# Zero padding the z product and the B and C product to full 128 x 128 tiles

## The chip, the cores and the metric

The kernel runs on one core of one Trainium2 chip. The metric is the device time of one launch in microseconds (us). A measured time is given as the median of several runs; a profile is one further execution, with its own time. PE is the matrix engine (TensorE), DVE the vector engine, ACT the scalar engine, POOL the GpSimd engine, SP the engine that here only issues DMAs. PEld stands for PE's weight loads.

## What is computed

The input is `x` of shape (4, 128, 64, 64). Layer 0 normalises it, passes it through a depthwise convolution, a GELU and a 1 x 1 product, and then through a selective state space model (Mamba). Layer 1 is attention with four heads over the 4096 pixels of each image, and a mixture of eight experts of which each pixel takes two. The change lies in the state space model. Its reference, cut to what matters:

```python
def _mamba(xc, in_proj_w, conv1d_w, conv1d_b, x_proj_w, ...):
    xz = u @ in_proj_w.T                      # (L, 32) by (32, 128)
    xin, z = jnp.split(xz, 2, axis=-1)        # 64 channels each
    xin = silu(depthwise_conv(xin, conv1d_w) + conv1d_b)
    x_dbl = xin @ x_proj_w.T                  # 2 + 16 + 16 columns
    dt, Bm, Cm = jnp.split(x_dbl, [R, R + N], axis=-1)
    delta = softplus(dt @ dt_proj_w.T + dt_proj_b)
    dA = jnp.exp(delta[..., None] * A)
    dBu = delta[..., None] * Bm[:, :, None, :] * xin[..., None]
    # h = dA * h + dBu, step by step over the pixels;  y = sum over n of h * C
    y = ... + D_skip * xin
    return y * silu(z) @ out_proj_w.T
```

The 128 channels of a pixel are cut into four chunks of 32, and the model runs on each chunk on its own. `in_proj_w` gives 64 channels to `xin` and 64 to `z` from the 32 of a chunk. All of this is in f32.

## The kernel before

**Tiles and stages.** An image of 4096 pixels is cut into eight blocks of 512 pixels (`BLK`). With four images that is 32 blocks. Channels lie on partitions. The four chunks are taken as two pairs, p = 0 and p = 1: pair p holds the channels on partitions 64p to 64p + 63, which are two chunks of 32, and one pair makes 2 x 64 = 128 rows of `xin`, of `z` and of the state. So the function `inputs(b, i, p)` (L659), which makes everything that the recurrence needs, runs 64 times, once for each image, block and pair.

**What `inputs` does.** It is a generator; each `yield` ends a stage.

- Stage one: PE makes the convolved input (`inxc` from `pairs`, two products that are summed in the PSUM tile `ps_Y`) and then `z` into the PSUM tile `ps_X`. For `z` it takes 64 rows of the weights `inz` and 64 rows of `xn`, those of the pair.
- Stage two: ACT makes `xin` (Silu of the first) and `zs` (Silu of the second).
- Stage three: PE makes the B and C columns (`wbc` from `xin`, 64 columns of weights, so 64 rows of the PSUM tile `pb`), and then `wdt` from `xin`.
- Stage four: ACT copies the 64 rows of `pb` to `bc`, which is sent to memory as `bcd`, and computes the softplus for `delta` in several steps (Abs, Exp, Ln, Relu). The stages after that let DVE finish `delta` and `du`.

A product of f32 operands is issued as two passes, so each call has two matmul instructions for `z` and two for B and C.

**What runs beside it.** The recurrence goes over units of two states: `fetched` brings the B or C rows from memory (`rows<-bcd`), `decayed` makes the factors on ACT (`da`), `driven` multiplies on DVE (`h<-rows,du`), `scan` runs the recurrence on DVE (`h<-da,state,h`), `read` multiplies with C on DVE (`hc`), and `turned_on` sums `hc` in PSUM with PE (`y<-ident,hc`). Attention of the image before runs in the same slots: PE makes scores (`sc<-qs,ks`, one pass each, 128 columns of weights), ACT takes exponentials (`pT<-sc`), and PE multiplies with the values one slot later (`av<-pT,v`, weights of 64 columns, two products beside each other in the two column halves).

**What sets the order.** Every instruction of the main loop goes through a small class `Queue` (its calls are recorded at L406), which chains each engine's instructions in the order of the program text. No scheduler moves them. In each slot the main loop issues, for PE, in this order: scores, one stage of a lane's task, `y` products, another stage, the `av` products, another stage. Two lanes, X and Y, hold tasks; `inputs` is in lane Y, and its products use the one PSUM buffer of each lane (`work("X")`, `work("Y")`). So the `pb` product waits until the last reader of lane X's buffer is done. In many calls with p = 0 that is the task that makes keys and queries (`closed`): its products `w_wkn` and `w_wqn` are read by DVE as `hi` and `lo`.

The weights are laid out by `_laid_out` on the host and loaded once at the start, `inz` and `wbc` on ACT's DMA queue.

Of the kernel before, what the change touches and what calls it, by code (L numbers as in the profile page):

```python
# [17 lines left out]
P = 128  # L18
C = 128
EPS = 1e-5  # L20
BLK = 512
NT = BLK // P
IMG = 64
DI = 64
NST = 16
# [11 lines left out]
def conv_mamba_attn_moe_kernel(ctx: ExitStack, tc: tile.TileContext, t: dict):  # L37
# [15 lines left out]
    def load(name, shape=None, src=None, eng=nc.sync, pool=const):  # L53
        src = t[name] if src is None else src
        w = pool.tile(list(shape or src.shape), F32, name=f"w_{name}")
        eng.dma_start(out=w, in_=src)
        return w
# [20 lines left out]
    inx, xdt, dtT, alog = (load(k, pool=scratch, eng=late) for k in ("inx", "xdt", "dtT", "alog"))  # L78
# [3 lines left out]
    inz, wbc, wout, projT = (load(k, eng=late) for k in ("inz", "wbc", "wout", "projT"))  # L82
# [14 lines left out]
    for j in range(4):  # L97
        r = slice(DI * (j % 2), DI * (j % 2) + DI)
# [313 lines left out]
    def mm(out, lhsT, rhs, start=True, stop=True):  # L412
        tensor.matmul(out, lhsT=lhsT, rhs=rhs, start=start, stop=stop)

    def summed(ps, terms):
        for i, (lhsT, rhs) in enumerate(terms):
            mm(ps, lhsT, rhs, i == 0, i == len(terms) - 1)
# [4 lines left out]
    def send(out, in_, slots=1):  # L422
        outgoing.append([slots, out, in_])
# [24 lines left out]
    def work(lane, shape=None):  # L448
        return ps_work.tile(shape or [P, BLK], F32, tag=f"work{lane}", name=f"ps_{lane}")

    def tmp(lane, name, shape=None):
        return side.tile(
            shape or [P, BLK], F32, tag=f"tmp{lane}", name=name, bufs=6 if lane == "X" else 4
        )
# [204 lines left out]
    def inputs(b, i, p):  # L659

        xn, pairs = xn_of[b, i], pairs_of[b, i]
        r = slice(DI * p, DI * p + DI)
        while held:
            yield
            yield
        held.add("in")
        ps = work("Y")
        summed(ps, [(inxc[:, j, :], pairs[:, p, 2 * j : 2 * j + BLK]) for j in range(2)])
        pz = work("X")
        mm(pz, inz[r, :], xn[r, 3 : 3 + BLK])  # L670
        yield
        xin = mix.tile([P, BLK], F32, name="xin", bufs=2)
        scalar.activation(xin, ps, AF.Silu, bias=cb)
        zs = mix.tile([P, BLK], F32, name="zs", bufs=4)
        scalar.activation(zs, pz, AF.Silu)
        yield

        pb = work("X")
        mm(pb[0:DI, :], wbc, xin)
        ps = work("Y")  # L680
        mm(ps, wdt, xin)
        yield
        held.clear()
        bc = tmp("Y", "bc")[0:DI, :]
        scalar.copy(bc, pb[0:DI, :])
        bcd = dram.tile([2, NST // 2, 2, 2 * BLK], F32, name="bcd", bufs=4)
        send(bcd.rearrange("c n k (m q) -> (c n k m) q", m=2), bc)

        e = tmp("Y", "e")
        scalar.activation(e, ps, AF.Abs, bias=dtb)  # L690
        scalar.activation(e, e, AF.Exp, scale=-1.0)
        ln = tmp("Y", "ln")
        scalar.activation(ln, e, AF.Ln, bias=1.0)
        delta = mix.tile([P, BLK], F32, name="delta", bufs=2)
        scalar.activation(delta, ps, AF.Relu, bias=dtb)
        yield
        yield

        du = mix.tile([P, BLK], F32, name="du", bufs=2)
        lost = du  # L700
        vector.tensor_scalar(lost, e, 1.0, -1.0, ALU.add, ALU.add)
        vector.tensor_sub(lost, e, lost)
        vector.tensor_add(ln, ln, lost)
        vector.tensor_add(delta, delta, ln)
        vector.tensor_mul(du, delta, xin)
        in_of[b, i, p] = xin, zs, delta, du, bcd
        done.add(("in", b, i, p))
        yield
# [603 lines left out]
    for k in range(-2, len(blocks)):  # L1312
        if 0 <= k:
            b, i = blocks[k]
            Y.append((("in", b, i, 1), inputs(b, i, 1), [("scan", *blocks[k - 1], 1)] if k else []))
        if k + 2 < len(blocks):
            b, i = blocks[k + 2]
            if k + 2 == 0 or i > 0:
                upper(k + 2)
        if 0 <= k + 1 < len(blocks):  # L1320
            b, i = blocks[k + 1]
            below = [("y0", b, i + 1)] if i < NB - 1 else []
            Y.append((("xn", b, i), conv(b, i), before(k + 1, 3) + below))
            Y.append((
                ("in", b, i, 0), inputs(b, i, 0),
                before(k + 1, 2) + ([("scan", *blocks[k], 0)] if k >= 0 else []),
            ))

        if 0 < k + 2 < len(blocks) and blocks[k + 2][1] == 0:
            upper(k + 2)  # L1330
# [113 lines left out]
def _laid_out(i):  # L1444
    import numpy as np

    f = {k: np.asarray(a) for k, a in i.items()}
    c0 = {k[len("L0_conv_") :]: a for k, a in f.items() if k.startswith("L0_conv_")}

    def col(a):  # L1450
        return a.reshape(-1, 1)

    def row(a):
        return a.reshape(1, -1)


    def twice(a):
        return np.repeat(a, 2, axis=0)

    z = np.zeros((P, P), np.float32)  # L1460
    inx, inz = z.copy(), z.copy()
    wout = np.zeros((P, 2, P), np.float32)
    wbc = np.zeros((P, 2, NST // 2, 2, 2), np.float32)
    xdt, dtT = np.zeros((4, P), np.float32), np.zeros((4, P), np.float32)
    for c in range(2):
        d = slice(c, P, 2)
        for p in range(2):
            s = slice(64 * p + 32 * c, 64 * p + 32 * c + 32)
            inx[s, d] = c0["in_proj_w"][:DI].T
            inz[s, d] = c0["in_proj_w"][DI:].T  # L1470
            wout[d, p, s] = c0["out_proj_w"].T

        wbc[d, c] = c0["x_proj_w"][2:].reshape(2, NST // 2, 2, DI).transpose(3, 1, 0, 2)
        xdt[2 * c : 2 * c + 2, d] = c0["x_proj_w"][:2]
        dtT[2 * c : 2 * c + 2, d] = c0["dt_proj_w"].T

    w = f["L1_attn_W_qkv"].reshape(C, NH, DH, 3)
    bw = f["L1_attn_b_qkv"].reshape(NH, DH, 3)
    wq, wk = np.zeros((C, 2, P), np.float32), np.zeros((C, 2, P), np.float32)
    bq, bk = np.zeros((P, 2), np.float32), np.zeros((P, 2), np.float32)  # L1480
    for h in range(NH):
        s = slice(64 * (h % 2), 64 * (h % 2) + DH)
        wq[:, h // 2, s], wk[:, h // 2, s] = w[:, h, :, 0], w[:, h, :, 1]
        bq[s, h // 2], bk[s, h // 2] = bw[h, :, 0], bw[h, :, 1]

        bk[64 * (h % 2) + DH, h // 2] = 1.0
    x = f["x"]
    laid = {
        "x": x.reshape(x.shape[0], C, -1),

        "xtok": x.reshape(x.shape[0], C, -1, P).transpose(0, 3, 2, 1).reshape(x.shape[0], P, -1),
        "gmat": np.kron(np.eye(C // 4), np.full((4, 4), 0.25)).astype(np.float32),
        "lnw": col(c0["ln_w"]), "lnb": col(c0["ln_b"]),
        "lcw": col(c0["lc_ln_w"]), "lcb": col(c0["lc_ln_b"]),
        "fc1w": c0["lc_fc1_w"].reshape(C, 9), "fc1b": col(c0["lc_fc1_b"]),
        "fc2T": c0["lc_fc2_w"].T, "fc2b": col(c0["lc_fc2_b"]),
        "inx": inx, "inz": inz,
        "cw": twice(c0["conv1d_w"]).T,
        "cb": col(twice(c0["conv1d_b"])),
        "xdt": xdt, "dtT": dtT, "dtb": col(twice(c0["dt_proj_b"])),  # L1500
        "wbc": wbc.reshape(P, -1), "alog": twice(c0["A_log"]),
        "dsk": col(twice(c0["D_skip"])), "wout": wout,
        "projT": c0["proj_w"].T, "projb": row(c0["proj_b"]), "skip": c0["skip_scale"],
        "wq": wq, "wk": wk, "wv": w[:, :, :, 2].reshape(C, C),
        "bq": bq, "bk": bk, "bv": row(bw[:, :, 2]),
        "wqn": w[:, :, :, 0].reshape(C, C), "wkn": w[:, :, :, 1].reshape(C, C),
        "bqn": col(bw[:, :, 0]), "bkn": col(bw[:, :, 1]), "bvc": col(bw[:, :, 2]),
        "wp": f["L1_attn_W_proj"], "bp": row(f["L1_attn_b_proj"]),
        "rw": f["L1_ffn_router_w"], "rb": f["L1_ffn_router_b"],
        "ew": f["L1_ffn_expert_w"].transpose(1, 0, 2), "eb8": f["L1_ffn_expert_b"],  # L1510
    }
    return {k: np.ascontiguousarray(a) for k, a in laid.items()}
# [17 lines left out]
```

## Time and profile before

| what | value |
|---|---|
| median of 3 runs | 5217.45 us (5217.27 to 5228.61) |
| the profiled execution: its own time | 5213.97 us |
| the profiled execution: span from first to last instruction | 5211.8 us |
| mean granted PE clock in it | 0.957 |
| `z`: matmul instructions, mean | 128, 664 ns |
| B and C: matmul instructions, mean | 128, 654 ns |
| `sc<-qs,ks`: matmul instructions, mean | 4096, 436 ns |
| `av<-pT,v`: matmul instructions, mean | 8192, 610 ns |

A group of instructions reads: line, engine, operation, output tile and input tiles, then for a matmul the used rows * columns of the array and the shape of the moving operand, the count, the busy time in us, the mean duration in ns, and the idle time of the engine before the group with the instructions that ended it. The timeline has start, duration and the same names, merged where equal instructions follow each other. The chain of waits lists, in order of time, what the end of the span is followed back to. Durations of matmuls overlap, because PE takes in the next one before the last has left; the distance from start to start is what one costs.

### The profile page before, as it was taken

How to read it: one execution, taken by the hardware profiler on the slowest of the kernel's cores; microseconds unless marked ns; L12 is line 12 of the kernel's file. 1: busy time of each engine (PE TensorE's matmuls, PEld its weight loads, DVE VectorE, ACT ScalarE, POOL GpSimd, SP SyncE). 2: the span in 40 equal slices, each digit the busy share in tenths (PEclk: the TensorE clock that was granted, in tenths of full speed). 3: DMA queues.
4: the chain of work that ended last, by engine and by line, in shares of the span. 5: the costliest groups of instructions: out<-in, count | busy, mean ns of one | idle time of the engine just before them, and what ended most of it. 6: DMA issues, size and time to landing. Idle time of an engine off the chain costs nothing.

```text
span 5211.8 us, 62608 instructions
## 1 busy us (share of the span) xinstructions
PE 4743.5 (91%) x20684; PEld 2298.3 (44%) x20684; DVE 3834.8 (74%) x5780; ACT 3749.6 (72%) x5700; POOL 423.0 (8%) x483
## 2 busy tenths in 40 slices
PE   4567899999999999899999999999999999999997
PEld 2333444444444444444444444444444444443443
DVE  6888767777788878888788887887788877751332
ACT  4456777788787787678888787778777787756543
POOL 1111111100000000001000000000000001000000
PEclk7678999999999999899999999999999999999998
DMA  4556567676766667767766667767766666754542
GB/s 126 180 186 207 210 208 244 227 236 242 234 225 228 230 223 239 244 231 246 258 228 226 233 224 231 259 229 253 264 233 228 219 229 219 265 179 156 185 130 72
DMA packets 451692, 1131.60 MB, mean 217 GB/s; under 512 B 51985, under 2 KB 135330, under 8 KB 451362
## 3 DMA queue, kind: packets, MB, share of 16 engines
q1 hardware_dynamic: 447296, 1125.96, 64.4%
q8 instruction: 166, 2.72, 0.2%
q10 hardware_dynamic: 4066, 1.57, 0.2%
q14 instruction: 164, 1.34, 0.1%
HBM read 967.12 MB, written 143.39 MB: 213 GB/s over the span
## 4 chain that ended last, share of the span: by engine, by line
PE 56%; DVE 17%; ACT 13%; DMA 6%; issue 5%; POOL 2%; SPq 1%; DVEq 0%; ACTq 0%; POOLq 0%
PE av L406 23%; PE sc L406 13%; PE ps_X L406 9%; DVE h L406 6%; PE ps_Y L406 5%; PE y L406 5%; ACT pT L406 4%; ACT L406 3%; DMA ks<-kd 2%; DVE hc L406 2%; ACT xt L406 1%; ACT e L406 1%; DMA rows<-bcd 1%; POOL rsX L406 1%; DVE stX L406 1%
## 5 line engine op out<-in xcount | busy, mean ns | idle before, releaser
L406 ACT ACTIVATE pT<-sc 128x1024 f32<-128x1024 f32 x2048 | 1985.0, 1023 | 941.0 <-PE sc L406 939.6
L406 PE MATMUL av<-pT,v 128*64 128x512 f32 x8192 | 2002.9, 610 | 11.4 <-DVE avs L406 11.4
L406 PE MATMUL sc<-qs,ks 128*128 128x512 f32 x4096 | 1294.3, 436 | 67.5 <-DMA ks<-kd 35.8
L406 DVE TENSOR_TENSOR_SCAN h<-da,state,h 128x1025 f32<-128x1025 f32 x512 | 1204.1, 2352 | 96.1 <-ACT h L406 62.5
L406 PEld LDWEIGHTS sc<-qs,ks 128*128 128x128 f32 x4096 | 701.9, 190 | 795.9 <-ACT pT L406 258.1
L406 PEld LDWEIGHTS av<-pT,v 128*64 128x64 f32 x8192 | 500.2, 137 | 846.4 <-issue 816.9
L406 ACT ACTIVATE da<-delta,amat 128x512 f32<-128x512 f32 x1024 | 743.1, 730 | 1.9
L406 PE MATMUL y<-ident,hc 128*128 128x128 f32 x4096 | 628.8, 285 | 64.5 <-DVE hc L406 64.5
L406 DVE TENSOR_TENSOR hc<-rows,h 128x1024 f32<-128x1024 f32 x512 | 624.2, 1219 | 15.8 <-PE y L406 5.9
L406 DVE TENSOR_TENSOR h<-rows,du 128x1024 f32<-128x1024 f32 x512 | 623.4, 1218 | 14.2 <-DMA rows<-bcd 14.1
L406 PEld LDWEIGHTS y<-ident,hc 128*128 128x128 f32 x4096 | 522.8, 147 | 236.9 <-issue 84.6
L406 ACT ACT_TABLE_LOAD x319 | 409.3, 1283 | 19.5 <-DVE zs L406 14.3
L406 POOL TENSOR_TENSOR rsX<-rsX,mhalf 128x4 f32<-128x4 f32 x92 | 203.7, 2214 | 2533.5 <-DVE rsX L406 2448.8
L406 POOL TENSOR_TENSOR rsY<-rsY,mhalf 128x4 f32<-128x4 f32 x100 | 130.6, 1306 | 2070.4 <-DVE shiftY L406 1558.8
L406 DVE TENSOR_TENSOR avs<-av,prev 128x512 f32<-128x512 f32 x96 | 66.1, 689 | 254.2 <-PE av L406 242.8
L406 PE MATMUL ps_X<-share,w_ew 128*128 128x512 f32 x432 | 217.0, 625 | 9.0 <-DVE share L406 8.8
L406 ACT ACTIVATE xt<-ps_Y,shiftY,rsY 128x128 f32<-128x128 f32 x380 | 143.9, 469 | 84.9 <-POOL shiftY L406 77.2
L406 DVE TENSOR_TENSOR share<-share,xf 128x1024 f32<-128x1024 f32 x128 | 155.9, 1218 | 20.5 <-DMA share<-sharesX 14.8
L406 ACT COPY state<-h 128x2 f32<-128x2 f32 x448 | 88.8, 198 | 92.8 <-DVE h L406 92.8
L406 DVE SCALAR_TENSOR_TENSOR cm<-y,w_fc1w,cm 128x512 f32<-128x512 f32 x195 | 144.9, 743 | 8.0 <-ACT y L406 4.5
L406 PE MATMUL ps_Y<-pairs,inxc 128*128 128x512 f32 x256 | 131.4, 638 | 15.0 <-DMA pairs<-xn 9.4
L406 PEld LDWEIGHTS ps_X<-share,w_ew 128*128 128x128 f32 x432 | 74.0, 191 | 149.4 <-issue 97.4
(248 smaller groups left out, 3435.9 us busy)
## 6 DMA issues: line engine op xcount, KB each, us to landing
rows<-bcd SPq DMA_DIRECT2D x1024, 512.0 KB
ks<-kd SPq DMA_DIRECT2D x192, 512.0 KB
qs<-qd SPq DMA_DIRECT2D x161, 512.0 KB
share<-sharesX SPq DMA_DIRECT2D x108, 512.0 KB
v<-vd SPq DMA_DIRECT2D x192, 256.0 KB
ks<-kd SPq DMA_DIRECT2D x128, 256.0 KB
avd<-avs SPq DMA_DIRECT2D x96, 256.0 KB
prev<-avd SPq DMA_DIRECT2D x96, 256.0 KB
```

The source lines that it names most:

```text
L406: return lambda *args, **kw: queued(op(*args, **kw))
```

## The change

`inz` had one weight matrix of 128 rows, of which the product took the 64 rows of the pair. It becomes two matrices of 128 rows, one for each pair, with zeros in the rows of the other pair, and the product takes all 128 rows of weights and of `xn`. `wbc` had 64 columns; 64 columns of zeros are added, and the product fills all 128 rows of `pb`. ACT still copies the first 64.

```diff
     def inputs(b, i, p):
 
         xn, pairs = xn_of[b, i], pairs_of[b, i]
-        r = slice(DI * p, DI * p + DI)
...
         pz = work("X")
-        mm(pz, inz[r, :], xn[r, 3 : 3 + BLK])
+        mm(pz, inz[:, p, :], xn[:, 3:])
...
         pb = work("X")
-        mm(pb[0:DI, :], wbc, xin)
+        mm(pb, wbc, xin)
         ps = work("Y")
         mm(ps, wdt, xin)
...
-    inx, inz = z.copy(), z.copy()
+    inx, inz = z.copy(), np.zeros((P, 2, P), np.float32)
     wout = np.zeros((P, 2, P), np.float32)
-    wbc = np.zeros((P, 2, NST // 2, 2, 2), np.float32)
+    wbc = np.zeros((P, 4, NST // 2, 2, 2), np.float32)
...
-            inz[s, d] = c0["in_proj_w"][DI:].T
+            inz[s, p, d] = c0["in_proj_w"][DI:].T
```

The loaded weights grow from 64 to 128 KB for `inz` and from 32 to 64 KB for `wbc`. The built program has the same instructions in the same order on every engine. The waits differ at PE: 74 of the `sc` products no longer wait on PE's own semaphore.

## The prediction

> **What bounds the kernel now.** I read the page's busy line and chain first, then the groups of PE by shape, then the order of time around one call of `inputs`, then the chain of waits there.
>
> ```profile
> PE 4743.5 (91%) x20684; PEld 2298.3 (44%) x20684; DVE 3834.8 (74%) x5780; ACT 3749.6 (72%) x5700; POOL 423.0 (8%) x483
> ...
> PE 56%; DVE 17%; ACT 13%; DMA 6%; issue 5%; POOL 2%; SPq 1%; DVEq 0%; ACTq 0%; POOLq 0%
> ```
>
> PE is busy 91% of the span, but carries only 56% of the chain that ended last. PE time saved is therefore not span saved until its place is known. The two groups that change are small, 128 instructions each (64 calls, two passes per f32 product):
>
> ```profile
> L406 PE MATMUL ps_X<-xn,w_inz 64*128 64x512 f32 x128 | 74.6, 664 | 0.0
> ...
> L406 PE MATMUL ps_X<-xin,w_wbc 128*64 128x512 f32 x128 | 73.0, 654 | 28.9 <-ACT zs L406 14.0 <-DVE lo L406 12.3 <-DVE stX L406 2.4
> ```
>
> Their durations are pipelined, so I use the distance between starts instead. PE in order of time, in a call for p = 0:
>
> ```profile
> 1060.98 1.88 PE L406 MATMUL ps_Y<-pairs,inxc 128*128 128x512 f32 x4
> 1062.79 1.12 PE L406 MATMUL ps_X<-xn,w_inz 64*128 64x512 f32 x2
> 1063.84 0.66 PE L406 MATMUL y<-ident,hc 128*128 128x128 f32 x4
> 1064.43 1.94 PE L406 MATMUL av<-pT,v 128*64 128x512 f32 x8
> 1066.29 1.19 PE L406 MATMUL sc<-qs,ks 128*128 128x512 f32 x4
> 1067.41 1.07 PE L406 MATMUL ps_X<-xin,w_wbc 128*64 128x512 f32 x2
> 1068.42 1.13 PE L406 MATMUL ps_Y<-xin,wdt 128*128 128x512 f32 x2
> 1069.38 0.60 PE L406 MATMUL y<-ident,hc 128*128 128x128 f32 x4
> 1069.91 0.65 PE L406 MATMUL av<-pT,v 128*64 128x512 f32 x2
> ```
>
> Inside the inxc row, passes start 0.429 us apart (single starts in the trace: 1060.977, 1061.406, 1061.836, 1062.265). The last one is followed by z's first pass only after 0.522. z's first pass takes 0.534, its second 0.518 until y, and y's first 0.165 instead of 0.108. The same four surcharges stand around w_wbc. These surcharges are what the change can remove.
>
> **What the Trainium skill says.** "TensorEngine Tiling (Array Packing)", Key Properties: changing the tiling mode, not only the tile, drains the TensorE. The trace agrees: 0.522 - 0.429 = 0.093 us appears exactly where 128*128 meets 64*128 or 128*64. "TensorE: Matmul & The Clock Gate", LDWEIGHTS (loading the stationary operand): a weight load lasts columns / 1.2 ns, whatever the rows. The trace agrees where the load is exposed: z's first pass is 0.105 us longer than 0.429 and w_wbc's, with 64 columns, 0.051. The same page, Why this matters for your kernels: a product with few rows takes as long as a full one. Here too: z's unburdened pass is 590 ns in the trace, inxc's 592. Padding itself costs no streaming time.
>
> **The change part by part, per call.**
> z, entry: the drain (0.093) and the exposed load (0.105) go: 0.198 us. z, exit: if y follows (p = 0, 24 of the 56 calls after 500 us), drain 0.090 and y's exposed load 0.057 go too, together 0.345. If av (128*64) follows (p = 1, 32 calls), that exit switch stays: 0.199.
> w_wbc behind a full-size product, PE not waiting (36 calls): entry drain 0.094 (sc's last pass 0.326 against 0.232), load 0.051, exit drain 0.093, wdt's load 0.105: 0.343. Where PE stalls for another engine before w_wbc (19 calls), entry is hidden in the stall and the wider load, 0.107 instead of 0.053, shows: 0.198 - 0.056 = 0.142. One call follows av: 0.05.
> PE time after 500 us: 24 x 0.345 + 32 x 0.199 + 36 x 0.343 + 19 x 0.142 = 29.7 us. The eight calls before 500 us run partly at half clock (passes 0.853 apart) and hold some 4 us more.
>
> Now where it lies. In 18 of the 24 p = 0 calls the chain runs through z and w_wbc:
>
> ```profile
> 2811.08 1.05 PE ps_X L406 x2
> 2812.13 0.59 PE y L406 x4
> 2812.72 1.87 PE av L406 x8
> 2814.58 1.07 PE ps_X L406 x2
> ...
> 2815.68 0.76 DVE hi L406
> ...
> 2816.47 0.76 DVE lo L406
> ...
> 2817.27 1.07 PE ps_X L406 x2
> 2818.34 1.07 PE ps_Y L406 x2
> ...
> 2819.43 0.70 ACT e L406
> ```
>
> z, y, av, the query product, DVE's hi and lo, w_wbc (it waits for the bank that lo frees), wdt, ACT's e: each waits for the one before. ACT idled 0.60 us before pT, 0.30 before bc and 0.48 before e, all for PE, so it follows when PE is early. Here 0.345 + 0.142 = 0.487 us per call is real.
>
> In most p = 1 calls it is not. ACT runs without a gap from the pT before z, through the table loads, xin, zs, e, ln and delta. DVE's chain does hang on PE (acc waited 7.92 us for it) but meets ACT again at the scan:
>
> ```profile
> 1559.37 0.69 DVE L406 TENSOR_TENSOR acc<-ps_X,acc 128x512 f32<-128x512 f32 x1 [7.92 <-PE ps_X L406]
> ...
> 1566.86 0.21 ACT L406 COPY h<-state 128x1 f32<-128x1 f32 x1
> ...
> 1567.20 2.35 DVE L406 TENSOR_TENSOR_SCAN h<-da,state,h 128x1025 f32<-128x1025 f32 x1
> ```
>
> The scan needs ACT's h, ended at 1567.07. So 0.1 us of the 0.542 can arrive. Then DVE runs to PE's next stall, which grows. Eleven calls look like this, at 0.1 each.
>
> Over all calls, the instructions that the chain holds carry: z before y 18 x 0.345 = 6.2; z before av 13 x 0.199 = 2.6; w_wbc not stalled 12 x 0.343 = 4.1; stalled 19 x 0.142 = 2.7; together 15.6 us. The calls before 500 us add 3.0 by the same count at their clock. Four calls whose ACT is close behind take back 1.3; the eleven above add 1.1. Sum 18.4. The chain knows one way at a time, so a second engine close behind takes some more; I take off 1.4, an estimate, and arrive at 17.
>
> Other edits. The weights grow by 64 and 32 KB, loaded once in the first 20 us on ACT's queue: 0 to 0.45 us (98 KB at the page's mean 217 GB/s); taken as 0. No instruction is added and each engine keeps its order; DVE and ACT read the same 64 rows of pb, at the same cost. The built program drops the wait on PE's own semaphore before 74 of the sc products; they waited for matmuls some 25 places back, long done, so I count 0. SP's issues keep their places.
>
> **Rivals.**
> 1. The forecast: 17 us along the chain. 5213.97 (5211.8 span and 2.2 around it) - 17 = 5197. The median of the runs is 3.5 above the profiled run, so 5200.5; own range 5192 to 5208.
> 2. All PE time counts: the PE row at 91% and clean PE-bound stretches between calls speak for it, ACT's gapless stretches against. 29.7 + 4 = 33.7 off: 5184.
> 3. Nearly all is swallowed: ACT, DVE or a rows transfer is late anyway and PE only stalls longer. For it: the 2.05 us PE stall in many p = 1 calls. Against: the p = 0 chain, where ACT idles for PE. About 5 us off: 5212.
> 4. The surcharges do not belong to the tile's size and stay: 0, so 5217. Against: they occur at w_wbc and z and not at inxc.
> 5. Slower: the clock gate. Where savings are hidden, PE idles longer; "TensorE: Matmul & The Clock Gate", Part 1, has a fixed window of about 3.4 us that halves the clock after idleness. The trace has this: between 1996 and 2003 us the granted clock is 0.76 after a 2.03 us stall, while 1566 to 1584, with 2.05, keeps 1.00. A window at half clock costs about 1.7 us of PE work. It decides from 10 new windows, which eat the gain; 20 make it slower by 17: 5234. Some 30 stalls of 2 us and more exist. Against: they grow by half a microsecond at most.
>
> **How the numbers follow.** Chances: forecast 0.55, all counts 0.17, swallowed 0.19, surcharges stay 0.02, clock 0.07. A change under 0.3%, 15.7 us, cannot be told from none. Of the forecast's 0.55, 0.33 lies beyond that (17 against 15.7, width 8), so faster 0.33 + 0.17 = 0.50; same 0.22 + 0.19 + 0.02 = 0.43; slower 0.07. The range 5184 to 5219 takes in rivals 2 to 4 and leaves out the clock case and the far ends.
>
> **What would show it.** Right: the w_inz rows read 128*128, their median falls from 693 to some 590 to 600 ns; inxc's four passes take 1.72 us to z instead of 1.81, z 0.86 instead of 1.05; PE busy falls by about 30 us while the span falls by half of that; p = 1 stalls of 2.05 us become about 2.5. Wrong: z's first pass still 0.534 (rival 4); span down by 30 (rival 2); PE idle up by as much as busy falls (rival 3); mean clock below 0.957 (rival 5).

## The result and the profile after

The changed kernel takes 5182.8 us (median of 6 runs, 5179.33 to 5187.62) against 5217.36 of the kernel before (5214.05 to 5228.61): ratio 0.9934, 95% interval 0.9924 to 0.9944, so 34 us less (29 to 40). The forecast was 17 us less, 5200.5, with a range that began at 5184. The direction was right, the size was half of what came. The profiled execution took 5183.13 us with a span of 5180.9, against 5213.97 and 5211.8; the mean granted clock is 0.957 in both.

The page of the changed kernel, busy time and the chain that ended last:

```profile
PE 4710.1 (91%) x20684; PEld 2321.9 (45%) x20684; DVE 3835.8 (74%) x5780; ACT 3745.7 (72%) x5700; POOL 423.1 (8%) x483
...
PE 59%; DVE 19%; ACT 10%; DMA 6%; issue 4%; POOL 2%; SPq 1%; DVEq 0%; ACTq 0%; POOLq 0%
```

PE lost 33.4 us of busy time (4743.5 to 4710.1), and the span lost 30.9. In this pair of executions nearly all of it reached the span. ACT's share of the chain fell from 13% to 10% and PE's rose from 56% to 59%. That fits an ACT that had been late together with PE and followed when PE came earlier; the shares alone do not show it.

The groups of PE by shape:

```profile
L406 PE MATMUL ps_X<-xin,w_wbc 128*128 128x512 f32 x128 | 71.1, 638 | 30.0 <-ACT zs L406 15.7 <-DVE lo L406 11.7 <-DVE stX L406 2.4
L406 PE MATMUL ps_Y<-xin,wdt 128*128 128x512 f32 x128 | 67.8, 612 | 0.0
L406 PE MATMUL ps_X<-xn,w_inz 128*128 128x512 f32 x128 | 67.7, 610 | 0.0
```

Both products now fill the array, and z's mean fell from 664 to 610 ns. In order of time, PE in the same p = 0 call as the one shown before:

```profile
1047.04 1.88 PE L406 MATMUL ps_Y<-pairs,inxc 128*128 128x512 f32 x4
1048.76 1.02 PE L406 MATMUL ps_X<-xn,w_inz 128*128 128x512 f32 x2
1049.61 0.60 PE L406 MATMUL y<-ident,hc 128*128 128x128 f32 x4
1050.14 1.94 PE L406 MATMUL av<-pT,v 128*64 128x512 f32 x8
```

From inxc to z it is 1.72 us (was 1.81), from z to y 0.85 (was 1.05), from y to av 0.53 (was 0.59). The surcharges are gone where they were expected to go. On the chain of waits of a p = 0 call with a query product:

```profile
2793.72 0.86 PE ps_X L406 x2
2794.58 0.44 PE y L406 x4
2795.02 1.87 PE av L406 x8
2796.88 1.07 PE ps_X L406 x2
...
2797.98 0.76 DVE hi L406
...
2798.76 0.76 DVE lo L406
...
2799.57 1.13 PE ps_X L406 x2
2800.70 0.87 PE ps_Y L406 x2
...
2801.59 0.69 ACT e L406
```

z takes 0.86 (was 1.05), y 0.44 (0.59), w_wbc behind its stall 1.13 (1.07: the wider weight load shows), wdt 0.87 (1.07): -0.19 - 0.15 + 0.06 - 0.20 = -0.48 us. This is the 0.487 of the forecast.

### The profile page after: what moved, and what is told of

Same layout as the page of the kernel before. It is cut to its first block, busy times and chain, and to the rows that moved or that the text cites. A ratio compares the mean times of both kernels' runs of the same rounds, so it can differ in the third digit from the quotient of the medians.

```text
span 5180.9 us, 62597 instructions
## 1 busy us (share of the span) xinstructions
PE 4710.1 (91%) x20684; PEld 2321.9 (45%) x20684; DVE 3835.8 (74%) x5780; ACT 3745.7 (72%) x5700; POOL 423.1 (8%) x483
## 4 chain that ended last, share of the span: by engine, by line
PE 59%; DVE 19%; ACT 10%; DMA 6%; issue 4%; POOL 2%; SPq 1%; DVEq 0%; ACTq 0%; POOLq 0%
PE av L406 25%; PE sc L406 14%; PE ps_X L406 9%; DVE h L406 6%; PE ps_Y L406 6%; PE y L406 5%; ACT pT L406 3%; ACT L406 2%; DVE hc L406 2%; DMA ks<-kd 2%; ACT xt L406 1%; DVE stX L406 1%; DVE du L406 1%; DMA rows<-bcd 1%; DVE cm L406 1%
```

## Where the forecast's missing half lies

**The scan did not wait for ACT.** The forecast let 0.1 of 0.542 us arrive in eleven p = 1 calls, because the scan on DVE started just behind an ACT copy into `h`. The timeline of the kernel before, first DVE and then ACT, in another such call (its z starts at 3003.06 us):

```profile
3013.53 0.69 DVE L406 TENSOR_TENSOR acc<-ps_X,acc 128x512 f32<-128x512 f32 x1 [8.33 <-PE ps_X L406]
...
3020.04 1.22 DVE L406 TENSOR_TENSOR h<-rows,du 128x1024 f32<-128x1024 f32 x1
3021.36 2.35 DVE L406 TENSOR_TENSOR_SCAN h<-da,state,h 128x1025 f32<-128x1025 f32 x1
```

```profile
3021.01 0.21 ACT L406 COPY h<-state 128x1 f32<-128x1 f32 x1
```

The same call of the changed kernel (z at 2982.3 us):

```profile
2992.34 0.69 DVE L406 TENSOR_TENSOR acc<-ps_X,acc 128x512 f32<-128x512 f32 x1 [7.87 <-PE ps_X L406]
...
2998.85 1.22 DVE L406 TENSOR_TENSOR h<-rows,du 128x1024 f32<-128x1024 f32 x1
3000.18 2.35 DVE L406 TENSOR_TENSOR_SCAN h<-da,state,h 128x1025 f32<-128x1025 f32 x1
```

```profile
3000.33 0.21 ACT L406 COPY h<-state 128x1 f32<-128x1 f32 x1
```

In the changed kernel the scan starts at 3000.18, before ACT's copy starts at 3000.33, so the copy is not what it waits for. By the kernel's text it is the copy that `prepared` makes for the next unit, into the other of two `h` buffers. In both kernels the scan starts 0.1 us behind DVE's own multiplication (3020.04 + 1.22 = 3021.26, and 2998.85 + 1.22 = 3000.07). DVE is a chain from `acc` on, and `acc` waits for PE. A PE that is 0.43 us earlier makes all of it 0.43 us earlier.

**A stall grew shorter, not longer.** Behind the scan DVE makes `bothX`, for which PE waits. PE's line in the changed kernel in that call:

```profile
3013.38 0.60 PE L406 MATMUL ps_X<-ident,bothX 128*16 128x128 f32 x4 [1.85 <-DVE bothX L406]
```

The bracket is the idle time ahead: 1.85 us. The same call of the kernel before:

```profile
3034.56 0.60 PE L406 MATMUL ps_X<-ident,bothX 128*16 128x128 f32 x4 [2.05 <-DVE bothX L406]
```

Relative to z, `bothX` comes 0.43 us earlier and PE arrives only 0.22 us earlier. The drain that was removed at z's entry lies ahead of z's start, so less than the whole gain of PE lies behind it, and 0.18 us is spent in a stall for pT at 14.4 us behind z. The stall therefore shrinks by 0.2 us. The forecast expected it to grow to 2.5.

That matters because of the clock. With z alone padded the stall stays at 2.05 us, and in one of those calls this follows, first PE's timeline, then the view by windows (window, its length, PE busy and instructions, granted clock, DMA share, GB/s):

```profile
3026.72 1.02 PE L406 MATMUL ps_X<-ident,bothX 128*16 128x128 f32 x4 [2.05 <-DVE bothX L406]
3027.39 2.06 PE L406 MATMUL sc<-qs,ks 128*128 128x512 f32 x4
3029.24 1.04 PE L406 MATMUL ps_Y<-ident,xt 128*128 128x128 f32 x4
```

```profile
3024.40:3026.80 2.40, 0.35 (x3) 0.99 0.64 246
3026.80:3030.20 3.40, 3.40 (x13) 0.51 0.30 89
3030.20:3033.60 3.40, 3.40 (x16) 1.00 0.89 270
```

For 3.4 us PE runs at half clock: sc takes 2.06 us for four passes, against some 1.2 elsewhere. Such a call takes 99.8 to 99.9 us instead of 98.1 to 98.4 (p = 1 calls from z to z), so each stretch costs 1.5 to 1.7 us. This suggested theory 5 below.

## The experiments

The theories, as the expectations number them. Theory 1: the gain is the removed tile-size switches, and they arrive in full in p = 1 calls too. Theory 2: the forecast's placing on the chain. Theory 3: the gain is the wait on PE's own semaphore that 74 `sc` products lose. Theory 4: it comes with the larger weights, by the layout or the start. Theory 5, added after the four half-padded kernels had been measured: a part of the gain is half-clock stretches that the shorter stall no longer starts.

| kernel | median us (runs) | ratio to before, 95% | us against before |
|---|---|---|---|
| changed kernel | 5182.80 (6) | 0.9934 (0.9924 to 0.9944) | -34.4 |
| z padded only | 5198.79 (6) | 0.9967 (0.9955 to 0.9979) | -17.2 |
| B and C padded only | 5201.27 (12) | 0.9981 (0.9973 to 0.9990) | -9.9 |
| p = 1 calls only | 5198.77 (5) | 0.9965 (0.9951 to 0.9978) | -18.2 |
| p = 0 calls only | 5206.41 (21) | 0.9985 (0.9979 to 0.9992) | -7.8 |
| larger weights, nothing padded | 5219.18 (14) | 0.9995 (0.9985 to 1.0005) | -2.6 |
| changed kernel, second comparison | 5188.60 (6) | 0.9938 (0.9922 to 0.9954) | -32.3 |
| before, wait filled | 5210.90 (22) | 0.9986 (0.9979 to 0.9993) | -7.3 |
| changed, wait filled | 5186.83 (6) | 0.9936 (0.9918 to 0.9953) | -33.4 |
| changed, router padded | 5179.91 (6) | 0.9933 (0.9917 to 0.9948) | -34.9 |
| changed, router padded, wait filled | 5173.09 (5) | 0.9916 (0.9902 to 0.9930) | -43.8 |
| changed kernel, third comparison | 5180.62 (6) | 0.9938 (0.9926 to 0.9950) | -32.3 |
| router padded, wait filled, again | 5175.95 (6) | 0.9931 (0.9918 to 0.9944) | -36.0 |

Each ratio is to the kernel before on the same chip. Its median there was 5217.36 us for the first row, 5213.97 for the four half-padded kernels, 5216.90 for the larger weights, the second comparison and the two kernels with the wait filled, 5215.99 for the next two and 5211.43 for the last two. The last column is that median times (ratio - 1); the plain difference of two medians departs from it by up to 5 us. Intervals are 3 to 9 us to each side, so the runs are read together with their traces.

**The two products apart.** Against the changed kernel:

```diff
-        mm(pb, wbc, xin)
+        mm(pb[0:DI, :], wbc[:, 0:DI], xin)
```

> Only the z product is padded; the B and C product is 64 columns wide as before. Theory 1, every removed tile-size switch arrives in full wherever no engine but PE is late: p = 1 calls 32 x 0.199 = 6.4 us, the 18 p = 0 calls with a query product 18 x 0.345 = 6.2, the calls before 500 us about 2; so -14.6 us against the kernel before (about 5203). Theory 2, the reading of the forecast (only what the chain of waits holds): -9 to -10. Theory 3, the gain comes from the waits on PE's own semaphore that 74 sc products lose: this kernel keeps these waits, so close to 0. Theory 4, a shift that comes with the larger weights alone: the same as the kernel with the larger weights and nothing padded.

```diff
-        mm(pz, inz[:, p, :], xn[:, 3:])
+        r = slice(DI * p, DI * p + DI)
+        mm(pz, inz[r, p, :], xn[r, 3:])
```

> Only the product for B and C is padded; z takes 64 rows as before. Theory 1: p = 1 calls 32 x 0.343 = 11.0 us, the 18 p = 0 calls with a query product 18 x 0.142 = 2.6, the calls before 500 us about 2; so -15.6 us (about 5202), and with the z part it adds up to the whole. Theory 2: -7 to -8. Theory 3: this kernel loses the 74 waits, so nearly all of the -34.

Measured: -17.2 for z and -9.9 for B and C. Theory 3 falls: with z alone padded, every wait of PE is as in the kernel before, and half of the gain is there; with B and C alone padded the 74 waits go, and far less than the whole comes. For z, theory 1's -14.6 lies within the interval (-23 to -11) and theory 2's -9 to -10 outside. For B and C it is the other way round: -15.6 lies outside (-14 to -5), and theory 2's -7 to -8 inside. Part of that is a wrong count in the expectations. They take 32 calls for p = 1; the traces have 28 behind 500 us, and the other four whose z is followed by av are p = 0. Counted rightly, theory 1 gives about -14 for either product, for B and C still at the edge of the interval. The times of this pair do not settle theory 1 against theory 2.

**The two halves of the calls apart.**

```diff
-        mm(pz, inz[:, p, :], xn[:, 3:])
+        if p == 1:
+            mm(pz, inz[:, p, :], xn[:, 3:])
+        else:
+            r = slice(DI * p, DI * p + DI)
+            mm(pz, inz[r, p, :], xn[r, 3:])
...
-        mm(pb, wbc, xin)
+        if p == 1:
+            mm(pb, wbc, xin)
+        else:
+            mm(pb[0:DI, :], wbc[:, 0:DI], xin)
```

> Both products are padded in the calls with p = 1 alone. Theory 1: 32 x 0.542 = 17.3 us and about 2 in the calls before 500 us, so -19 us (about 5198). Theory 2: z before av 2.6, w_wbc unstalled 4.1, eleven calls at 0.1 and 1.5 early, so -8 to -9 (about 5209). Theory 3: about half of the waits go, -17 whichever p it is.

The other kernel of this pair is the same with `p == 0`.

> Both products are padded in the calls with p = 0 alone. Theories 1 and 2 agree: 18 calls with a query product x 0.487 = 8.8 us, about 2 in the calls before 500 us, nothing in the p = 0 calls without one, where ACT's exponentials are late: -11 us (about 5206). If the calls without a query product count too, 24 x 0.487 + 2 = -13.7. With the p = 1 kernel it should add up to the whole -34; a sum short of it by more than 3 us leaves a part that neither call explains.

Measured: -18.2 for p = 1 (-25 to -11) and -7.8 for p = 0 (-11 to -4). The -8 to -9 of the forecast's placing lies outside the first interval; theory 1's -19, or -17 with 28 calls, lies inside. The -11 expected for p = 0 is at the edge of the second. The sum, -26, is 8 us short of the whole, more than the 3 us that were allowed for. The traces decide the placing more sharply. The distance from one call's z to the next call's z repeats to 0.1 us where the clock stayed at full speed. The table gives the medians of its difference to the same call with nothing padded, over calls behind 1350 us that are free of half-clock stretches in both (the shortest of several traces where there are several). That leaves 14 or 15 calls for p = 0; for p = 1 it leaves 7, 9, 10, 3 and 13 from the first row to the last:

| padded | p = 0 calls | p = 1 calls |
|---|---|---|
| z only | -0.34 | -0.20 |
| B and C only | -0.14 | -0.34 |
| p = 1 calls only | -0.09 | -0.44 |
| p = 0 calls only | -0.40 | -0.04 |
| both, all calls | -0.50 | -0.53 |

The forecast worked out 0.345 and 0.199 for z, 0.142 and 0.343 for B and C. All four costs arrive, in p = 1 as in p = 0. (The -0.09 in calls that are not padded is the entry drain of the next call's z, which lies ahead of that z's start. The -0.04 should be the same and rests on three calls.) The p = 0 calls without a query product are not in the median; they go from 44.4 to 44.3 us, swallowed, as the forecast had it.

**The control.** Both products narrow, on the larger weights, by the two edits above together.

> Only the larger weights are loaded; both products use the same 64 rows and 64 columns as before. Theory 1 (the gain is the removed tile-size switches): 0, within 2 us. Theory 4 (the layout of the weights or the start of the kernel brings part of the 34 us): -3 to -6, as the span of the changed kernel was already 5 us ahead at 500 us.

Measured: -2.6, with an interval from -8 to +3 (its median is 2 us above that of the kernel before). No gain can be seen in it, and theory 4 is not needed. The lead of the changed kernel at 500 us does not come with the weights either: z of the ninth call starts at 509.4 us in this kernel's trace, at 508.1 in that of the kernel before and at 502.7 in that of the changed kernel.

**The changed kernel on the same chip, and the wait filled.**

> The changed kernel unaltered, on the chip of the three others of this batch. The two halves of each split added up to -27 and -26 us, the change was -34.6. If theory 1 is enough, it shows about -27 to -30 here too. If the two halves are short because a stall of PE before the transposes of bothX (2.05 us in kernels where p = 1 is not fully padded, 1.82 where it is) starts a half-clock stretch in 2 to 10 of 12 such calls, and in 0 of 10 where it is shorter (theory 5): -30 to -36, with a spread over the runs of under 10 us where the kernel before has over 15.

```diff
         ps = work(lane)
+        if lane == "X":
+            mm(ps[:, 0:256], ident, xf[:, 0:256])
         for j in range(NT):
             tensor.transpose(ps[0 : 2 * NE, j * P : (j + 1) * P], both[:, j, :], ident)
```

This is made to the kernel before and to the changed kernel.

> The kernel before, with one more product of PE in lane X (256 columns, its result is overwritten), put where PE waits for bothX; every one of these 27 waits is at least 0.4 us, so its 0.43 us delays nothing. Theory 5 (half-clock stretches after the 2.05 us stall cost 1.5 to 1.7 us each and come in 2 to 10 of 12 calls): the stall becomes 1.62, none of these stretches is left, -4 to -12 us, and a smaller spread. Without theory 5: 0, or up to +3.

> The changed kernel with the same product in the wait for bothX. Theory 5: ten of its stalls are 1.82 us and start no half-clock stretch already; only the four or five of 2.0 to 2.7 us can gain, so 0 to -5 us against the changed kernel, and the gain of the fill is smaller here than in the kernel before. Without theory 5: 0 against the changed kernel.

Measured: -32.3 for the changed kernel; -7.3 (-11 to -4) for the kernel before with an added product that computes nothing; -33.4 for the changed kernel with it, 1 us from the one without. Extra work on the busiest engine makes the kernel before faster. For the changed one no gain can be seen, though with 8 to 9 us to each side one of a few us would not show. The trace of the kernel before with its wait filled:

```profile
3025.72 0.70 PE L406 MATMUL ps_X<-xf,ident 128*128 128x256 f32 x2
3027.83 0.61 PE L406 MATMUL ps_X<-ident,bothX 128*16 128x128 f32 x4 [1.40 <-DVE bothX L406]
```

The stall is 1.40 us (1.62 was expected), and the transposes come no later: 31.51 us behind z, as in the kernel before. p = 1 calls free of stretches take the same 98.4 us as before, so nothing but the clock is seen to change. Counted over the traces of all kernels, by the length of the stall ahead of the `bothX` transposes and whether a half-clock stretch falls on it or starts within 4 us of its beginning:

| kernels | stall 1.9 to 2.1 us: with a stretch | 1.6 to 1.9 us | 0.3 to 1.6 us |
|---|---|---|---|
| p = 1 not fully padded, unfilled (5 traces) | 29 of 62 | none such | 0 of 43 |
| p = 1 fully padded, unfilled (5 traces) | 9 of 14 | 1 of 47 | 0 of 40 |
| wait filled (4 traces) | 2 of 4 | none such | 4 of 58 |

The four of the last row lie at the end of the kernel, where PE was at half clock already when the stall began. Stalls of 2.4 to 4.1 us are not in the table (37 of 58 with a stretch). Some 12 stalls in a kernel were 2.05 us and half of them started a stretch. Ten of the 12 became 1.82, where nearly none does. By this count it is 29 / 62 x 10 x 1.5 = 7 us, an estimate; filling the wait, which shortens all 12, measured 7.3.

What looks like chance is the place of a stall on a grid. In each of the 14 traces all changes of the granted clock lie within 6 ns of a grid of 3.413 us, and where this grid begins differs from one execution to the next. Of the 62 stalls, 31 had 1.95 us or more inside one window of the grid, and 29 of these started a stretch; the other 31 had less, and none did. A stall of 1.82 us cannot put 1.95 us into any window. How many of the stalls start a stretch differs from one execution to the next (2, 5, 6, 6 and 10 in the five traces), and this is one source of the spread between executions: 26 us over 35 executions of the kernel before on this chip, 16 over 22 with the wait filled.

**The same for the router.** Padding its two narrow products as well:

```diff
-        both = routed("both", 2 * NE)
+        flat = wide_both[lane]
+        both = flat[:, 0 : 2 * NE * NT].rearrange("p (j n) -> p j n", n=2 * NE)
...
-            tensor.transpose(ps[0 : 2 * NE, j * P : (j + 1) * P], both[:, j, :], ident)
+            tensor.transpose(
+                ps[:, j * P : (j + 1) * P], flat[:, 2 * NE * j : 2 * NE * j + P], ident
+            )
...
-        mm(ps, eb8, prT[0:NE, :])
+        mm(ps, eb8, prT)
```

`wide_both` is one tile for each lane, 176 columns, with zeros behind its 64; `eb8` gets rows of zeros up to 128. ACT then copies 128 rows of `prT` instead of 16 (0.59 us instead of 0.58).

> The changed kernel, with the two narrow products of the router padded as well: the transposes of bothX take 128 columns of weights, and the product of prT with w_eb 128 rows. By theory 1 the exit of the prT product goes (0.516 - 0.429 = 0.087 us drain, 0.341 - 0.230 = 0.111 us load of the next sc), 0.198 us in each of 32 calls, -6 us against the changed kernel if PE decides there; the bothX exit is worth nothing (0.028 + 0.313 us until the second sc pass now, 0.109 + 0.230 at full size). A p = 1 call free of half-clock stretches should take 97.7 us instead of 97.9. If those 0.2 us are swallowed, 0 and 97.9.

> The same with the product of 256 columns in the wait for bothX. By theories 1 and 5 together -6 us for the padding and 0 to -5 for the few stalls of 2.0 to 2.7 us that are left, so -6 to -11 against the changed kernel, about 5175. If both are swallowed, 0.

Measured: -34.9 without and -43.8 with the filled wait. Without it, the 6 us that were expected beyond the changed kernel do not show in the time: it stands 0.5 to 2.6 us beyond the three comparisons of the changed kernel, with 8 us to each side. The p = 1 calls free of stretches take 97.7 us in both (97.9 in the changed kernel), as expected from 0.198 us. In the trace of the version with both, the transposes fill the array and the stall is short:

```profile
3007.38 0.70 PE L406 MATMUL ps_X<-xf,ident 128*128 128x256 f32 x2
3009.30 0.66 PE L406 MATMUL ps_X<-ident,bothX 128*128 128x128 f32 x4 [1.22 <-DVE bothX L406]
```

Beside the changed kernel on one chip:

> The changed kernel unaltered, beside the version with the padded router and the filled wait on one chip: -28 to -36 us against the kernel before, as in its two earlier comparisons.

> The version with the padded router and the filled wait: if its gain is 6 us for the router and up to 5 for half-clock stretches, it stands 6 to 11 us below the changed kernel on the same chip; if the earlier 9 us came from the chip, 0.

Measured: -32.3 and -36.0, 4.7 us between the medians. Both of its comparisons lie lower than all three of the changed kernel (0.9916 and 0.9931 against 0.9934, 0.9938, 0.9938), but on one chip the intervals overlap. It is faster than the kernel before by 36 to 44 us; that it beats the changed kernel is likely and not settled by the times. What is settled is its 0.2 us in a p = 1 call.

## Why the prediction was half right

**Right.** The surcharges belong to the size of the tile. The cost of each switch, the PE time in all (33.4 us of busy time against 29.7 + 4), the swallowed calls without a query product, and the 0.487 us of a p = 0 call all came out. Padding costs no streaming time (z's two passes take 0.85 us from start to start), and the loads nothing that can be seen. The Trainium skill, "TensorEngine Tiling (Array Packing)", Key Properties, says that a change of the tiling mode drains the TensorE; the 0.09 us that went with each removed switch agrees.

**The step that failed** is the placing of the p = 1 calls: "The scan needs ACT's h, ended at 1567.07. So 0.1 us of the 0.542 can arrive." The scan needs DVE's own multiplication, and that hangs on PE. The forecast credited p = 1 with 2.6 + 4.1 + 1.1 = 7.8 us. If its 28 calls behind 500 us all gain like those in the table, 28 x 0.53 = 14.8 came. The 1.3 us taken back for four calls with a near ACT and the 1.4 for other near engines rest on the same reading, and by the same argument were not due. 7.0 + 2.7 = 9.7 us. (The forecast's "p = 1, 32 calls" are 28 calls with p = 1 and four with p = 0; its sum of PE time is the same either way.)

**The step that was missing** is the clock, and its sign was wrong. Rival 5 saw that stalls of about 2 us sometimes start a half-clock stretch, but took it that stalls grow. The commonest one shrank from 2.05 to 1.82 us, below what starts a stretch.

How much that brought is known only roughly. The filled wait measured 7.3 us for some 12 stalls (4 to 11), and the change shortens ten of them. The mean granted clock of the runs points to less. Over the runs of the kernel before, on each of four chips, 0.001 more of it goes with 3 us less. The runs of the changed kernel stand 0.0011 and 0.0012 above those of the kernel before on the two chips where both have it on record, which makes 3 to 4 us; the kernel before with the wait filled stands 0.0028 above, which makes 8.

**A term that may be too small** is the 3.0 us for the calls before 500 us. The z of the ninth call starts at 508 to 511 us in the three traces with both products narrow, and at 499 to 504 in the seven with both padded. How much of this lead is switches and how much is clock is not shown.

Together: 17 + 9.7 makes 27 us of PE time that arrives, and 3 to 7 us for the clock makes 30 to 34, against 34.4, 32.3 and 32.3 measured. That rival 2's time, 5184, was met is partly luck: it lets all PE time arrive, also that of the calls that swallow it, and leaves out the clock. One thing stays open. The two halves by p add up to 26 us and not to 34. Neither of their traces has the lead at 500 us (509.5 and 508.8), and neither product alone lacks it (502.0 and 502.2), but these are single executions. The p = 1 half should hold the clock's part too, and its trace indeed has no stretch at its ten stalls of 1.8 us; the -18.2 of five runs, with 7 us to each side, is too coarse to say whether it does.

## What to carry to other kernels

A small product between full-size ones should be padded to the full tile where its operand can hold the zeros: here the switches around one product cost 0.14 to 0.34 us and the zeros nothing. A false dependency is found by asking whether the instruction in question could ever start before the one it is said to need; two instructions that stand next to each other in a trace are no proof, and a buffer with two copies is the usual trap. And look at the stalls of the matrix engine near 2 us before costing an edit: in this kernel, moving ten of them from 2.05 to 1.82 us was worth an estimated 3 to 7 us beside 27 for the edit itself.

## What was not expected of the hardware

Half-clock stretches come in units of 3.4 us, at a granted clock of 0.5. They started at 29 of 62 stalls of 1.9 to 2.1 us in the kernels where that stall is common, and at 1 of 47 of 1.6 to 1.9 us, counted at one place in the program. Which of them do goes with how they lie on the 3.413 us grid on which the clock changes: between 500 and 4500 us in the 14 traces, each of the 246 windows at full clock in which PE was busy less than 40% was followed by one at half clock, and so were 114 of 399 between 40% and 60%, and 3 of 15137 above. A stall of 2.05 us leaves 40% of a window if it falls wholly into it, one of 1.82 us leaves 47%.

The Trainium skill, "TensorE: Matmul & The Clock Gate", Part 1, gives one idle window of about 3.4 us as what brings the half clock. The length of the stretches agrees, but a stall well under one window was enough here. Filling 0.43 us of a 2.05 us stall with a product whose result is thrown away made the kernel before 7.3 us faster (3.7 to 11.0).
